# Keys and values of four tiles at once, from thirds of the context on four row groups of the tensor engine

## The chip, the cores and the metric

The kernel runs on one core of one Trainium2 chip. The metric is the device time of one launch in microseconds (us), taken as the median of three runs. TensorE (PE in the profile, with its weight loads as PEld) multiplies, ScalarE (ACT), VectorE (DVE) and GpSimd (POOL) do the rest, and SyncE (SP) issues the DMAs. All data are float32. Each float32 matmul shows as two PE instructions in the trace.

## The reference, cut to what matters

A stack of four layers runs over 128 sequences of 64 tokens with 128 channels. Each layer is a gated cross-attention to a context of 64 tokens with 96 channels, followed by a gated feed-forward part. Layers 0, 1 and 3 have attention of this form:

```python
# heads of 64 channels: 8 in layers 0 and 1, 16 in layer 3
q = norm(x) @ Wq          # 128 -> heads * 64
k = ctx @ Wk              #  96 -> heads * 64
v = ctx @ Wv              #  96 -> heads * 64
a = softmax(q k^T * 64 ** -0.5)      # within one sequence; layer 3 has a null key and value besides
x = x + tanh(gate) * ((a v) @ Wo + bo)
```

Layer 2's attention has 16 heads of 8 channels with biases. Layer 0's feed-forward part mixes 16 experts, layer 2's mixes 32, layer 1's is one 128x128 product in the frequency domain (it is folded into layer 1's attention here), layer 3's is a low-rank MLP.

## The kernel before

The 8192 tokens are 64 tiles of 128. A tile is two sequences. `x` stays in SBUF for the whole kernel; so does the transposed context, `ctxT`, with 96 rows of channels, a row of ones below them, and 8192 columns of tokens.

The stages run one after the other: layer 0's attention (`l0x`), its experts (`l0f`), layer 1's attention with its feed-forward part (`l1x`), layer 2's attention (`l2x`) and experts (`l2f`), layer 3's attention (`l3x`) and MLP (`l3f`). Within a stage the order of every engine is written out by hand: engines are wrapped in `InOrder` (line 158), so each of them executes in the order of the Python calls. DMAs that `load` and `weights` issue on SP are not in that written order. The last steps of a stage call `ahead().step()`, which emits the first steps of the next stage.

`l0x` and `l1x` come from `cross` (line 382). They take the tiles in 32 pairs. Function `periods` (line 354) runs period i, and in it each entry `(lag, f)` of a plan for pair i + lag. In one period of `l0x` the plan gives this order:

- `turn` of pair i-2 (line 284): transposes of the attention weights into two PSUM banks, which ACT copies to `aT`
- `qk` of pair i (line 207): queries (`psq`) and keys (`psk`) by two banks each, copied by ACT with a scale to `qT` and `kT`
- `power` and `divide` of pair i-1 (lines 269 and 273): the exponential on ACT, then on DVE the sums `den` and their reciprocal `rec`, then on POOL the product
- `add` of pair i-3 (line 400): the output projection into a bank `pso`, which DVE takes up in one instruction that adds it to `x`
- `turned` of pair i+1 (line 347): transposes of the normalised tokens (`psx`), copied by ACT
- `values` of pair i (line 219): values into two banks `psv`, copied by ACT
- `scores` and `less` of pair i (lines 231 and 244), then `second` of pair i-2 (line 292): the product of weights and values, which ACT copies to `oT`

`l1x` has besides, between `turned` and `values`, the transposes and the product of the feed-forward part; DVE takes up that product's bank (`ps_l1f`) right after `pso`. `l3x` (line 1146) has the same period for each half (8 heads) of each pair, 64 periods in all; there the projection of the first half is copied by ACT (`y`), that of the second is added by DVE (line 1231), and the null key and value bring two small steps, `null` and `turn_null`.

PSUM has eight banks. `bank` (line 63) hands out single ones from four, and `banks` (line 66) pairs from two pairs; scores and `o` take pairs, and all else takes single ones:

```python
return psum.tile([P, 512], F32, tag="one", name=name, bufs=4)
```

## Time and profile before

| What | us |
|---|---|
| median of three runs | 3196.38 |
| lowest and highest | 3195.07, 3200.67 |
| profiled execution, its own time | 3195.21 |
| span in its profile, first to last instruction | 3193.4 |
| PE busy | 3028.7 |
| DVE busy | 1938.7 |
| ACT busy | 1586.8 |
| POOL busy | 1259.6 |

The profiled execution took 1.8 us more than its span, and 1.2 us less than the median. By the stretches of the trace, `l0x` runs to about 366 us, `l0f` to 930, `l1x` to 1309, `l2x` to 1638, `l2f` to 2401, `l3x` to about 3120 and `l3f` to the end. The PE column of such a table says how long an engine had an instruction under way; it does not say whether the next one could have begun sooner.

### The profile page before, as it was taken

What the parts mean: (1) busy time and instruction counts of PE and PEld (TensorE: products, weight loads), DVE (VectorE), ACT (ScalarE), POOL (GpSimd) and SP (SyncE); (2) the same over time, 40 slices, a digit from 0 to 9 for tenths busy, and PEclk for the clock granted to TensorE, in tenths of its full rate; (3) what the DMA queues carried; (4) which work ended last, traced back from release to release, by engine and by line L of the source; (5) the groups of instructions that cost most, each with busy time, mean ns of one, the idle gap of its engine ahead of it and who ended that gap; (6) DMA issues with size and microseconds to landing.
All of it is one profiled execution on the core that took longest, in us unless ns stands there. A gap on an engine that the chain in (4) does not pass through costs nothing.

```text
span 3193.4 us, 80225 instructions
## 1 busy us (share of the span) xinstructions
PE 3028.7 (95%) x34146; PEld 2023.2 (63%) x34146; DVE 1938.7 (61%) x4589; ACT 1586.8 (50%) x2790; POOL 1259.6 (39%) x1441
## 2 busy tenths in 40 slices
PE   8999999999989999788889999999999999999998
PEld 7887644444448888565654444444447888888883
DVE  5666566666536667699864444444445666666674
ACT  5666432222236666688823233233225666666665
POOL 3434211111014444787624444444442333333343
PEclk9999999999989999999999999999999999999999
DMA  5000455654610000000034534534520000000001
GB/s 150 2 2 2 113 128 116 137 120 112 141 50 2 3 3 2 29 3 2 3 71 90 107 74 87 107 77 84 107 54 13 3 2 2 3 2 2 2 2 54
DMA packets 85672, 165.03 MB, mean 52 GB/s; under 512 B 7393, under 2 KB 16225, under 8 KB 84353
## 3 DMA queue, kind: packets, MB, share of 16 engines
q1 hardware_dynamic: 85314, 159.90, 22.2%
q8 instruction: 268, 4.39, 0.6%
q14 instruction: 90, 0.74, 0.1%
HBM read 154.10 MB, written 5.77 MB: 50 GB/s over the span
## 4 chain that ended last, share of the span: by engine, by line
PE 78%; DVE 12%; ACT 6%; POOL 2%; issue 2%; DMA 0%; SPq 0%; DVEq 0%; ACTq 0%; POOLq 0%
PE psgu_l2f L166 11%; PE psqkv_l0f L166 10%; PE psy_l2f L166 5%; PE pso_l3x L166 4%; PE psq_l3x L166 4%; PE psv_l3x L166 4%; PE psy_l0f L166 4%; PE psk_l3x L166 4%; PE sc_l3x L166 2%; PE psa_l3x L166 2%; PE o_l3x L166 2%; PE psq_l1x L166 2%; PE psv_l1x L166 2%; PE psk_l1x L166 2%; PE psv_l0x L166 2%; PE pso_l1x L166 2%
## 5 line engine op out<-in xcount | busy, mean ns | idle before, releaser
L166 PE MATMUL psgu_l2f<-xT_l2f,w_l2f 128*128 128x512 f32 x1088 | 512.7, 594 | 1.6 <-DVE uw_l2f L166 1.5
L166 POOL TENSOR_TENSOR h_l2f<-uw_l2f,sl_l2f 128x512 f32<-128x512 f32 x256 | 324.9, 1269 | 417.3 <-DVE uw_l2f L166 417.3
L166 ACT ACTIVATE sl_l2f<-psgu_l2f 128x512 f32<-128x512 f32 x272 | 162.4, 597 | 483.8 <-PE psgu_l2f L166 483.6
L166 DVE TENSOR_TENSOR uw_l2f<-psgu_l2f,wb_l2f 128x512 f32<-128x512 f32 x256 | 176.2, 689 | 370.5 <-ACT sl_l2f L166 370.5
L166 PEld LDWEIGHTS psgu_l2f<-xT_l2f,w_l2f 128*128 128x128 f32 x1088 | 202.7, 190 | 239.4 <-issue 225.2
L166 PE MATMUL psqkv_l0f<-xs_l0f,w_l0f 128*128 128x512 f32 (+1 forms) x1024 | 350.2, 599 | 1.8 <-DVE xs_l0f L166 1.7
L166 PE MATMUL psy_l2f<-h_l2f,w_l2f 128*128 128x512 f32 x544 | 277.5, 592 | 0.0
L166 PEld LDWEIGHTS psqkv_l0f<-xs_l0f,w_l0f 128*128 128x128 f32 (+1 forms) x1024 | 124.4, 163 | 187.2 <-issue 177.2
L166 POOL TENSOR_TENSOR at_l3x<-s_l3x,rec_l3x 128x1024 f32<-128x1024 f32 x64 | 121.7, 1902 | 189.4 <-PE psv_l3x L166 96.4
L166 PEld LDWEIGHTS psy_l2f<-h_l2f,w_l2f 128*128 128x128 f32 x544 | 103.3, 190 | 130.2 <-issue 128.2
L166 DVE TENSOR_REDUCE den_l3x<-s_l3x 128x16 f32<-128x1040 f32 x64 | 79.1, 1236 | 155.5 <-ACT s_l3x L166 155.5
L166 POOL TENSOR_SCALAR rs_l0f<-mv_l0f 128x4 f32<-128x4 f32 x16 | 15.2, 950 | 378.4 <-DVE mv_l0f L166 378.4
L166 DVE TENSOR_TENSOR xs_l0f<-wb_l0f,xT_l0f 128x1024 f32<-128x1024 f32 x128 | 151.8, 1215 | 5.1 <-DMA wb_l0f<-wrow_l0f 2.6
L166 POOL TENSOR_TENSOR x<-x,gbias_b 128x256 f32<-128x256 f32 (+1 forms) x80 | 67.9, 849 | 212.9 <-DVE ln_xn_l1x L166 109.3
L166 POOL TENSOR_TENSOR s_l2x<-s_l2x,m_l2x 128x1024 f32<-128x1024 f32 x64 | 120.4, 1903 | 51.8 <-DVE m_l2x L166 29.3
L166 PE MATMUL psq_l3x<-xT_l3x,w_l3x 128*128 128x256 f32 x512 | 136.8, 390 | 2.3
L166 PE MATMUL psk_l3x<-ctxT,w_l3x 96*128 96x256 f32 x512 | 132.8, 381 | 0.0
L166 DVE TENSOR_TENSOR s_l3x<-sc_l3x,maskf_m 128x512 f32<-128x512 f32 x128 | 82.5, 686 | 82.5 <-PE sc_l3x L166 82.5
L166 PE MATMUL pso_l3x<-w_l3x,oT_l3x 128*128 128x128 f32 x1024 | 130.2, 275 | 0.8 <-ACT oT_l3x L166 0.8
L166 PEld LDWEIGHTS pso_l3x<-w_l3x,oT_l3x 128*128 128x128 f32 x1024 | 126.8, 192 | 4.5 <-ACT oT_l3x L166 1.1
L166 PE MATMUL psv_l3x<-w_l3x,ctxT 96*64 96x256 f32 x1024 | 124.6, 385 | 0.0
L166 PE MATMUL psy_l0f<-mix_l0f,w_l0f 128*128 128x512 f32 x256 | 117.1, 611 | 2.0 <-DVE mix_l0f L166 2.0
(564 smaller groups left out, 6789.3 us busy)
## 6 DMA issues: line engine op xcount, KB each, us to landing
wb_l0f<-wrow_l0f SPq DMA_DIRECT2D x256, 256.0 KB, 6.2
wb_l2f<-wrow_l2f SPq DMA_DIRECT2D x128, 512.0 KB, 8.6
out_dram<-x SPq DMA_DIRECT2D x16, 256.0 KB, 2.6
w_l2f<-in_l2f_dram SPq DMA_DIRECT2D x1, 3280.0 KB, 10.3
w_l0f<-in_l0f_dram SPq DMA_DIRECT2D x1, 2120.0 KB, 28.3
w_l3x<-in_l3x_dram SPq DMA_DIRECT2D x1, 2113.0 KB, 8.6
x<-in_x_dram SPq DMA_DIRECT2D x1, 2048.0 KB, 18.7
ctxT<-in_ctxT_dram SPq DMA_DIRECT2D x1, 1536.0 KB, 24.2
```

The costliest lines, as they stand in the source:

```text
L166: got = getattr(self.eng, op)(*args, **kwargs)
```

## The change

Three things change for `l0x`, `l1x` and `l3x`. The context lies in SBUF as `ctx4`: each group of four tiles has its first tile's channels on partitions 0 to 31, the second's on 32 to 63, and so on, and the 96 channels are three thirds of 32, one after another along the free dimension. The weights of keys and values are cut the same way and repeated on the four sets of 32 partitions, so they are three times as wide. The new class `Keys` makes the keys, or the values, of four tiles in one burst: for each third, four matmuls of 32 rows each, one for each tile, on the four row groups, adding up in four PSUM banks. The burst takes all four single banks at once, and then ACT copies the four. Keys are made in odd periods and values in even ones, after `scores` and `less`.

In `l3x` the order of the halves is changed so that two pairs share a burst. Its value and output weights are a new tile `l3v`, loaded at the start of `l2f`. `l2x` needs whole columns of the context, so it loads them again from DRAM in pieces of 512 tokens (`held`), for its mean over the context (now 16 reductions in place of 4) and for its keys and values. The two scales of layer 3's queries and keys are one, on the queries. At the start, the weights of the keys are loaded ahead of those of the queries. The row of ones is not loaded.

```diff
-XA = dict(q=512, k=512, v=512, o=512)
+XA = dict(q=512, k=3 * 512, v=3 * 512, o=512)
...
-    "l3x": Cols(q=1024, k=1024, v=1024, o=1024, gn=1, nv=1, hot=8 * 16),
+    "l3x": Cols(q=1024, k=3 * 1024, gn=1, nv=1, hot=8 * 16),
+    "l3v": Cols(v=3 * 1024, o=1024),
...
-    ctxT = const.tile([DC + 1, NTOK], F32, name="ctxT")
+    ctx4 = const.tile([P, NG, 3, P], F32, name="ctx4")
...
     load(ident, "cst", 0, P)
-    load_w0("q")
     load_row(0, 8 + DM)
     load_ctx(0, 512)
     load_w0("k")
+    load_w0("q")
...
+    class Keys:
...
+        def burst(self, name, pl, bufs, blocks):
+
+            ps = [bank(f"ps{name}_{self.name}_{t}") for t in range(4)]
+            for block in blocks:
+                for c in range(3):
+                    for t in range(4):
+                        for r_out, c_out, lhsT, rhs in block(slice(32 * t, 32 * t + 32), c):
+                            self.pe.matmul(ps[t][r_out, c_out], lhsT=lhsT, rhs=rhs, start=c == 0, stop=c == 2)
+            got = pl.tile([P, 4, 512], F32, tag=f"{name}4", name=f"{name}4_{self.name}", bufs=bufs)
+            for t in range(4):
+                self.act.copy(got[:, t, :], ps[t])
+            return got
+
+        def keys(self):
+
+            def block(j):
+                def parts(rows, c):
+                    c0 = c * self.width + self.off + j * P
+                    return [(slice(0, P), slice(j * P, (j + 1) * P), self.w["k"][rows, c0:c0 + P], ctx4[rows, self.g, c, :])]
+                return parts
+            self.k = self.burst("k", self.wk, 1, [block(j) for j in range(4)]).rearrange("p t (j q) -> p t j q", q=P)
+
+        def values(self):
+
+            def block(b):
+                def parts(rows, c):
+                    c0 = c * self.width + self.off
+                    return [(slice(r * 64, (r + 1) * 64), slice(b * 256, (b + 1) * 256), ctx4[rows, self.g, c, b * SQ:(b + 1) * SQ],
+                             self.w["v"][rows, c0 + r * 256:c0 + (r + 1) * 256]) for r in range(2)]
+                return parts
+            self.v = self.burst("v", self.late, 2, [block(b) for b in range(2)]).rearrange("p t (b k) -> p t b k", b=2)
...
             plan = [
-                (-2, lambda p: H[p].turn()), (1, norm), (0, lambda p: H[p].qk(0, N[p].xT)),
-                (0, lambda p: H[p].qk(1, N[p].xT)), (-1, lambda p: H[p].power()), (2, lambda p: N[p].moments(xp[p])),
-                (-1, lambda p: H[p].divide()), (-3, add), (1, lambda p: N[p].turned()), (0, lambda p: H[p].values()),
-                (0, lambda p: H[p].scores()), (0, lambda p: H[p].less()), (-2, lambda p: H[p].second()),
+                (-2, lambda p: H[p].turn()), (1, norm), (0, lambda p: H[p].queries(N[p].xT)),
+                (-1, lambda p: H[p].power()), (2, lambda p: N[p].moments(xp[p])),
+                (-1, lambda p: H[p].divide()), (-3, add), (1, lambda p: N[p].turned()),
+                (0, lambda p: H[p].scores()), (0, lambda p: H[p].less()), (1, of_two(lambda g: KV[g].keys())),
+                (0, of_two(lambda g: KV[g].values())), (-2, lambda p: H[p].second()),
             ]
...
+            def context(k, g):
+                load(held[k][g % 2][0:DC, :], "ctxT", g * 512, (g + 1) * 512, slice(0, DC))
...
+            for g in range(NG):
+                k = "kv"[g // 2 % 2]
+                dve.tensor_reduce(cm[:, 8 * g:8 * g + 8], held[k][g % 2].rearrange("p (b k) -> p b k", k=SQ), AX.X, ALU.add)
+                if g + 4 < NG:
+                    context(k, g + 4)
...
+            l3v = ctx.enter_context(opened("l3v")).tile([P, LAY["l3v"].n], F32, name="w_l3v")
+            load(l3v, "l3v", 0, LAY["l3v"].n)
...
+        def of(i):
+            return 2 * (i // 4) + i % 2, i // 2 % 2
...
-                (0, lambda i: H[i].qk(0, N[i // 2].xT)), (0, lambda i: H[i].qk(1, N[i // 2].xT)),
+                (0, lambda i: H[i].queries(N[of(i)[0]].xT)),
                 (-1, lambda i: H[i].power()), (2, first(moments)), (4, make), (-1, divide),
-                (-3, project), (1, first(turned)), (0, lambda i: H[i].values()),
-                (0, lambda i: H[i].scores()), (0, lambda i: H[i].less()), (-2, lambda i: H[i].second()),
+                (-3, project), (1, first(turned)), (0, lambda i: H[i].scores()), (0, lambda i: H[i].less()),
+                (1, of_two(lambda n: KV[n].keys())), (0, of_two(lambda n: KV[n].values())), (-2, lambda i: H[i].second()),
```

More of the change, by code (lines that the diff above doesn't have):

```diff
@@ L96, in load_ctx @@
     def load_ctx(lo, hi):
-        load(ctxT[0:DC, lo:hi], "ctxT", lo, hi, slice(0, DC))
+        g0, g1 = lo // 512, hi // 512
+        load(ctx4[:, g0:g1].rearrange("p g c q -> p (g c q)"), "ctx4", g0 * 384, g1 * 384)
     w0 = wpool.tile([P, LAY["l0x"].n], F32, tag="wx", name="w_l0x")
@@ L126, in load_rest @@
             load_ctx(lo, hi)
-        load(ctxT[DC:DC + 1, :], "ctxT", 0, NTOK, slice(DC, DC + 1))
     tg = const.tile([P, 8], F32, name="tg")
@@ L192, in run, with __init__ @@
                 pass
+    class Keys:
+        def __init__(self, engines, wk, late, w, off, width, g, name):
+            self.act, self.pe = engines[1], engines[3]
+            self.wk, self.late, self.w, self.off, self.width, self.g, self.name = wk, late, w, off, width, g, name
+        def burst(self, name, pl, bufs, blocks):
[24 more added lines that the diff above has]
+            self.v = self.burst("v", self.late, 2, [block(b) for b in range(2)]).rearrange("p t (b k) -> p t b k", b=2)
@@ L194, in flamingo_kernel, with __init__ @@
     class Heads:
-        def __init__(self, engines, wk, late, w, off, p, name, qs, ks, mask=None, null=None):
+        def __init__(self, engines, wk, late, w, off, p, name, scale, kv, mask=None, null=None):
             self.dve, self.act, self.pool, self.pe, _ = engines
-            self.home = dict.fromkeys(("aT", "oT", "v", "s"), late)
+            self.home = dict.fromkeys(("aT", "oT", "s"), late)
             self.wk, self.w, self.off, self.p, self.name = wk, w, off, p, name
-            self.scale, self.mask, self.null = dict(q=qs, k=ks), mask, null
+            self.scale, self.kv, self.mask, self.null = scale, kv, mask, null
@@ L204, in new, with queries @@
         def new(self, tag, shape, bufs=1):
             return self.home.get(tag, self.wk).tile(shape, F32, tag=tag, name=f"{tag}_{self.name}", bufs=bufs)
-        def qk(self, half, xT):
-            tok, w, name = self.p * 256, self.w, self.name
-            if half == 0:
-                self.T = {k: self.new(f"{k}T", [P, 4, 256]) for k in "qk"}
-            for k, K, rhs in (("q", P, xT), ("k", DC, ctxT[0:DC, tok:tok + 256])):
-                ps = bank(f"ps{k}_{name}_{half}")
+        def queries(self, xT):
+            self.qT = self.new("qT", [P, 4, 256])
+            for half in range(2):
+                ps = bank(f"psq_{self.name}_{half}")
@@ L213, in qk @@
                 for i in range(2):
                     c0 = self.off + (half * 2 + i) * P
-                    self.pe.matmul(ps[:, i * 256:(i + 1) * 256], lhsT=w[k][0:K, c0:c0 + P], rhs=rhs, start=True, stop=True)
-                self.act.activation(self.T[k][:, 2 * half:2 * half + 2, :].rearrange("p a b -> p (a b)"), ps, AF.Copy,
-                                    scale=self.scale[k])
-        def values(self):
-            self.v = v = self.new("v", [P, 4, 256], bufs=3)
-            for half in range(2):
-                ps = bank(f"psv_{self.name}_{half}")
-                for i in range(2):
-                    b0 = self.p * 256 + (half * 2 + i) * SQ
-                    for r in range(2):
-                        self.pe.matmul(ps[r * 64:(r + 1) * 64, i * 256:(i + 1) * 256], lhsT=ctxT[0:DC, b0:b0 + SQ],
-                                       rhs=self.w["v"][0:DC, self.off + r * 256:self.off + (r + 1) * 256],
-                                       start=True, stop=True)
-                self.act.copy(v[:, 2 * half:2 * half + 2, :].rearrange("p a b -> p (a b)"), ps)
+                    self.pe.matmul(ps[:, i * 256:(i + 1) * 256], lhsT=self.w["q"][:, c0:c0 + P], rhs=xT, start=True, stop=True)
@@ L231, in scores @@
+                self.act.activation(self.qT[:, 2 * half:2 * half + 2, :].rearrange("p a b -> p (a b)"), ps, AF.Copy,
+                                    scale=self.scale)
         def scores(self):
@@ L240, in scores @@
                             self.pe.matmul(sc[b * 64:(b + 1) * 64, r, (t * 4 + j) * 64:(t * 4 + j + 1) * 64],
-                                           lhsT=self.T["q"][rows, j, c0:c0 + SQ], rhs=self.T["k"][rows, j, c0:c0 + SQ],
+                                           lhsT=self.qT[rows, j, c0:c0 + SQ],
+                                           rhs=self.kv.k[rows, 2 * (self.p % 2) + t, j, b * SQ:(b + 1) * SQ],
                                            start=True, stop=True)
@@ L301, in second @@
                                 self.pe.matmul(o[hi * 64:(hi + 1) * 64, r, c0:c0 + 64],
-                                               lhsT=self.v[rows, t * 2 + b, j * 64:(j + 1) * 64],
+                                               lhsT=self.kv.v[rows, 2 * (self.p % 2) + t, b, j * 64:(j + 1) * 64],
                                                rhs=self.aT[rows, t, j, b * 64:(b + 1) * 64], start=True, stop=True)
@@ L345, in scaled, with turned @@
                                        ALU.subtract, ALU.mult)
-        def turned(self, tag="xT", scale=1.0):
+        def turned(self, tag="xT", scale=1.0, bufs=1):
             ps = bank(f"psx_{self.name}")
@@ L350, in turned, with of_two @@
                 self.pe.transpose(ps[:, t * P:(t + 1) * P], self.xn[:, t, :], ident)
-            self.xT = self.new(tag, [P, 256])
+            self.xT = self.new(tag, [P, 256], bufs)
             self.act.activation(self.xT, ps[:, 0:256], AF.Copy, scale=scale)
+    def of_two(f):
+        return lambda i: f(i // 2) if i % 2 == 0 else None
     def periods(n, plan):
@@ L391, in cross @@
             W[nxt] = weights(nxt)
-            H = [Heads(engines, wk, late, w, 0, p, f"{key}_{p}", 0.125, 1.0, mask=mask) for p in range(NP)]
+            KV = [Keys(engines, wk, late, w, 0, 512, g, f"{key}_{g}") for g in range(NG)]
+            H = [Heads(engines, wk, late, w, 0, p, f"{key}_{p}", 0.125, KV[p // 2], mask=mask) for p in range(NP)]
             N = [Norm(engines, wk, f"{key}_{p}") for p in range(NP)]
@@ L451, in mix @@
                     del M[p]
-                plan[9:9] = [(-5, lambda p: M[p].turned("xT2")), (-6, mix)]
-                plan[6:6] = [(-4, begin)]
+                plan[8:8] = [(-5, lambda p: M[p].turned("xT2")), (-6, mix)]
+                plan[5:5] = [(-4, begin)]
                 plan[2:2] = [(-5, lambda p: norm(p, M, "b1f", "ln_xn2"))]
@@ L758, in l2_cross @@
             yield True
-            cm = wk.tile([DC + 1, NB], F32, name="cm", bufs=1)
-            for c in range(4):
-                b0 = slice(c * NB // 4, (c + 1) * NB // 4)
-                dve.tensor_reduce(cm[:, b0], ctxT[:, c * NTOK // 4:(c + 1) * NTOK // 4].rearrange("p (b k) -> p b k", k=SQ),
-                                  AX.X, ALU.add)
-                yield True
+            held = {k: [wk.tile([DC + 1, 512], F32, name=f"ctx_{k}{i}", bufs=1) for i in range(2)] for k in "kv"}
+            for k in "kv":
+                for i in range(2):
+                    gps.memset(held[k][i][DC:DC + 1, :], 1.0)
+            def context(k, g):
+                load(held[k][g % 2][0:DC, :], "ctxT", g * 512, (g + 1) * 512, slice(0, DC))
+            cm = wk.tile([DC + 1, NB], F32, name="cm", bufs=1)
+            for g in range(4):
+                context("kv"[g // 2], g)
+            yield True
+            for g in range(NG):
[3 more added lines that the diff above has]
+                    context(k, g + 4)
+                if g % 4 == 3:
+                    yield True
+            for g in range(2):
+                context("k", g)
+                context("v", g)
             dve.tensor_scalar(cm, cm, 1.0 / SQ, None, ALU.mult)
@@ L810, in qk @@
                 ps = bank(f"psk_l2x_{g}")
-                mat.matmul(ps, lhsT=w["k"][0:DC + 1, :], rhs=ctxT[:, g * 512:(g + 1) * 512], start=True, stop=True)
+                mat.matmul(ps, lhsT=w["k"][0:DC + 1, :], rhs=held["k"][g % 2], start=True, stop=True)
+                if g + 2 < NG:
+                    context("k", g + 2)
                 kT = sg[g]["k"] = wk.tile([P, 512], F32, tag="kT", name=f"kT_l2x_{g}")
@@ L861, in values @@
                 for b in range(4):
-                    b0 = u * 256 + b * SQ
+                    b0 = u % 2 * 256 + b * SQ
                     for r in range(2):
-                        mat.matmul(ps[r * 64:(r + 1) * 64, b * 64:(b + 1) * 64], lhsT=ctxT[:, b0:b0 + SQ],
+                        mat.matmul(ps[r * 64:(r + 1) * 64, b * 64:(b + 1) * 64], lhsT=held["v"][u // 2 % 2][:, b0:b0 + SQ],
                                    rhs=wv[0:DC + 1, r], start=True, stop=True)
                 su[u]["psv"] = ps
+                if u % 2 == 1 and u // 2 + 2 < NG:
+                    context("v", u // 2 + 2)
             def place(u):
@@ L1125, in l2_ffn @@
             yield False
+            l3v = ctx.enter_context(opened("l3v")).tile([P, LAY["l3v"].n], F32, name="w_l3v")
+            load(l3v, "l3v", 0, LAY["l3v"].n)
+            W["l3x"].update(views(l3v, "l3v"))
             with opened("l2f_2", 2) as wk2, opened("l2f_wb", 4, RIGHT) as wbp:
@@ L1179, in l3_cross @@
         H, sn, y, anT = {}, {}, {}, {}
+        def of(i):
+            return 2 * (i // 4) + i % 2, i // 2 % 2
         def of_pair(f):
-            return lambda i: f(i // 2) if i % 2 == 0 else None
+            return lambda i: f(of(i)[0]) if of(i)[1] == 0 else None
         moments = of_pair(lambda p: N[p].moments(xp[p], twice=True))
         scaled = of_pair(lambda p: N[p].scaled(xp[p]))
-        turned = of_pair(lambda p: N[p].turned(scale=w["gn"]))
+        turned = of_pair(lambda p: N[p].turned(scale=w["gn"], bufs=2))
         for f in (moments, scaled, turned):
@@ L1194, in l3_cross @@
             NO = [Norm(engines, wk, f"l3x_{p}o") for p in range(NP)]
+            KV = [Keys(engines, wk, wk, w, 512 * (n % 2), 1024, n // 2, f"l3x_{n}") for n in range(2 * NG)]
             def null(i):
-                p, hf = divmod(i, 2)
+                p, hf = of(i)
                 if hf == 0:
@@ L1203, in null @@
                     actor.copy(sn[p].rearrange("p t h -> p (t h)"), ps[:, 0:32])
-                H[i] = Heads(engines, wk, wk, w, 512 * hf, p, f"l3x_{p}_{hf}", rs, rs, mask=mask, null=sn[p][:, :, 8 * hf:8 * hf + 8])
+                H[i] = Heads(engines, wk, wk, w, 512 * hf, p, f"l3x_{p}_{hf}", rs * rs, KV[i // 2], mask=mask,
+                             null=sn[p][:, :, 8 * hf:8 * hf + 8])
             def divide(i):
-                p, hf = divmod(i, 2)
+                p, hf = of(i)
                 H[i].divide(ans[p % 2][:, :, 8 * hf:8 * hf + 8])
             def turn_null(i):
-                p, hf = divmod(i, 2)
+                p, hf = of(i)
                 if hf == 1:
@@ L1220, in project @@
             def project(i):
-                p, hf = divmod(i, 2)
+                p, hf = of(i)
                 more = [(anT[p][:, t * P:(t + 1) * P], nvo) for t in range(2)] if hf == 1 else (None, None)
@@ L1235, in out_ @@
             def out_(i):
-                p, hf = divmod(i, 2)
+                p, hf = of(i)
                 if hf == 1:
@@ L1411, in _o_rows, with _thirds @@
     return m.reshape(2, 2, 2, 64, P).transpose(0, 3, 2, 1, 4).reshape(P, 512)
+def _thirds(m):
+    return np.tile(m.reshape(3, 32, -1).transpose(1, 0, 2).reshape(32, -1), (4, 1))
 def _layout(i):
@@ L1416, in _layout @@
     f["x"] = i["x"].reshape(NT, P, DM).transpose(1, 0, 2).reshape(P, NT * DM)
-    f["ctxT"] = np.concatenate([i["ctx_768"].reshape(NTOK, DC).T, np.ones((1, NTOK), np.float32)])
+    f["ctxT"] = i["ctx_768"].reshape(NTOK, DC).T
+    f["ctx4"] = i["ctx_768"].reshape(NG, 4, P, 3, 32).transpose(1, 4, 0, 3, 2).reshape(P, NG * 3 * P)
     for name, key in (("m0", "mask_BxS2_bk0"), ("m1", "mask_BxS2_bf1")):
         f[name] = i[key].reshape(NT, 2, SQ).transpose(1, 0, 2).reshape(2, NT * SQ)
-    f["l0x"] = _pack("l0x", q=i["L0_xattn_W_q"], k=i["L0_xattn_W_k"], v=_v_cols(i["L0_xattn_W_v"]),
+    f["l0x"] = _pack("l0x", q=i["L0_xattn_W_q"], k=_thirds(i["L0_xattn_W_k"]), v=_thirds(_v_cols(i["L0_xattn_W_v"])),
                      o=_o_rows(i["L0_xattn_W_o"]))
-    f["l1x"] = _pack("l1x", q=i["L1_xattn_Wq"], k=i["L1_xattn_Wk"], v=_v_cols(i["L1_xattn_Wv"]),
+    f["l1x"] = _pack("l1x", q=i["L1_xattn_Wq"], k=_thirds(i["L1_xattn_Wk"]), v=_thirds(_v_cols(i["L1_xattn_Wv"])),
                      o=_o_rows(i["L1_xattn_Wo"]))
@@ L1458, in _layout @@
     nk, nv = i["L3_xattn_null_kv"]
-    f["l3x"] = _pack("l3x", q=i["L3_xattn_Wq"], k=wkv[:, :1024],
-                     v=np.concatenate([_v_cols(wkv[:, c:c + 512]) for c in (1024, 1536)], axis=1),
-                     o=np.concatenate([_o_rows(wo[c:c + 512]) for c in (0, 512)], axis=1),
+    f["l3v"] = _pack("l3v", v=_thirds(np.concatenate([_v_cols(wkv[:, c:c + 512]) for c in (1024, 1536)], axis=1)),
+                     o=np.concatenate([_o_rows(wo[c:c + 512]) for c in (0, 512)], axis=1))
+    f["l3x"] = _pack("l3x", q=i["L3_xattn_Wq"], k=_thirds(wkv[:, :1024]),
                      gn=i["L3_xattn_g_norm"][:, None], nv=np.concatenate([nv, nv])[:, None], hot=hot.reshape(P, -1))
```

## The prediction, made before the changed kernel was run

> **What bounds the kernel now.** I read the page first, then the stages, then one period of `l0x` in order of time.

> ```profile
> PE 3028.7 (95%) x34146; PEld 2023.2 (63%) x34146; DVE 1938.7 (61%) x4589; ACT 1586.8 (50%) x2790; POOL 1259.6 (39%) x1441
> ```

> By stretches of the span (length, then busy time of PE, PEld, DVE, ACT, POOL with instructions, PE clock, DMA share, GB/s), and by groups of PE instructions:

> ```profile
> 40.00:335.00 295.00, 288.58 (x5062) 246.62 (x5062) 185.95 (x397) 190.33 (x311) 120.62 (x150) 0.99 0.02 6
> ```

> ```profile
> L166 PE MATMUL psv_l0x<-w_l0x,ctxT 96*64 96x256 f32 x512 | 62.3, 385 | 0.0
> ```

> PE is under way in 288.6 of 295 us of `l0x`, and the values found PE idle for 0.0 us. No transfer matters there (DMA share 0.02). So the stage is a row of matmuls. The period says how long each takes, and where the other engines stand (start, duration, engine):

> ```profile
> 202.15 1.01 ACT L166 COPY oT_l0x<-o_l0x 128x1024 f32<-128x1024 f32 x1 [1.51 <-PE o_l0x L166]
> ...
> 203.05 1.08 ACT L166 COPY aT_l0x<-psa_l0x 128x512 f32<-128x512 f32 x2
> ...
> 203.75 1.03 PE L166 MATMUL psk_l0x<-ctxT,w_l0x 96*128 96x256 f32 x4
> ...
> 204.01 0.63 ACT L166 ACTIVATE qT_l0x<-psq_l0x 128x512 f32<-128x512 f32 x1
> ...
> 204.61 1.03 PE L166 MATMUL psq_l0x<-xT_l0x,w_l0x 128*128 128x256 f32 x4
> ...
> 206.34 1.95 PE L166 MATMUL pso_l0x<-w_l0x,oT_l0x 128*128 128x128 f32 x16
> 206.54 0.60 ACT L166 ACTIVATE kT_l0x<-psk_l0x 128x512 f32<-128x512 f32 x1 [0.27 <-PE psk_l0x L166]
> ...
> 207.04 1.05 ACT L166 ACTIVATE s_l0x<-s_l0x 128x1024 f32<-128x1024 f32 x1
> ...
> 208.12 1.22 DVE L166 TENSOR_REDUCE den_l0x<-s_l0x 128x16 f32<-128x1024 f32 x1 [1.96 <-ACT s_l0x L166]
> 208.13 0.38 PE L166 MATMUL psx_l0x<-cst_t,ln_xn_l0x 128*128 128x128 f32 x2
> ...
> 208.44 1.95 PE L166 MATMUL psv_l0x<-w_l0x,ctxT 96*64 96x256 f32 x16
> ...
> 209.61 0.39 DVE L166 SCALAR_TENSOR_TENSOR x<-pso_l0x,tg,x 128x256 f32<-128x256 f32 x1
> ...
> 210.32 1.16 PE L166 MATMUL sc_l0x<-kT_l0x,qT_l0x 64*64 64x64 f32 x64
> ```

> Four PE instructions of 256 columns take 203.75 to 204.61, so 0.216 each; sixteen of 128 columns take 206.34 to 208.13, 0.112 each. Keys are 8 x 0.216 = 1.73 us of a period, values 208.44 to 210.32 = 1.88. The start of `sc` recurs every 10.39 us here; read the same way, every 11.06 in `l1x`, and by turns 10.39 and 11.54 (mean 10.97) in `l3x`. The second thing to see: DVE frees the bank of `pso` only at 210.00, 1.5 us after PE has gone on to the values. Today nobody waits for it, since other single banks are free.

> **The change part by part: PE.** A burst of keys is 4 blocks x 3 thirds x 4 tiles = 48 matmuls, 96 instructions of 128 columns; of values, 2 x 3 x 4 x 2 = 48, so 96 of 256 columns. What they cost hangs on overlap. The trace has row groups of 32 at work:

> ```profile
> 3120.20 1.14 PE L166 MATMUL psh_l3f<-pT_l3f,w_l3f 32*128 32x512 f32 x8
> ...
> 1340.74 1.12 PE L166 MATMUL sc_l2x<-kb_l2x,qT_l2x 32*64 32x256 f32 x32
> ...
> 3185.47 1.72 PE L166 MATMUL psy_l3f<-w_l3f,qT_l3f 32*128 32x128 f32 x32 [0.69 <-ACT qT_l3f L166]
> ```

> Eight of `psh` end in 1.14 us, where a pair of the same length takes 1.02 (`psy_l2f`): four run at once. The 32 of `sc_l2x`, with two column groups besides, end in 1.12 = 4 waves of 0.216 and a tail: eight at once. So keys are 24 waves x 0.112 = 2.69, values 12 x 0.216 = 2.59, and 0.2 us for filling and changing over: about 2.83 for either. [...] With the rows, PE alone has 2 x (1.73 + 1.88) = 7.22 us per two periods before and 2.69 + 2.59 + 0.4 = 5.68 after: -1.54 x 64 = -99 us. No more is in it: 96 rows in four row groups of 32 are three quarters of the passes.

> **ACT and PSUM.** The copies are as many and as large as before, and two scales on ACT become plain copies: nothing. [...] A burst needs all four single banks within its first four matmuls, so each earlier user must have been taken up, `pso` among them; and its four copies all begin after its end. Behind them on ACT, in written order, stand `oT`, two of `aT`, two of `qT`, then the exponential; behind that on DVE `den`, `rec` and the taking up of `pso`; and then the next burst. Laid out from the end of a burst in `l0x`, by the starts above: 0.25 to the first copy; four copies 4 x 0.48 = 1.92; `oT` 0.90; `aT` 0.96; `qT` 2 x 0.50; the exponential 1.08 until `den`; `den` to the end of the adding 1.88; 0.1 to PE. That is 8.1 us. PE meanwhile has 10.39 - 1.73 - 1.88 = 6.8 us of work, so it stands for 1.3 us in each period. Loop: 8.1 + 2.83 = 10.92 against 10.39, +0.53 x 32 = +17 us. In `l1x`, `ps_l1f` is taken up 0.39 us after `pso`: 8.5 + 2.83 = 11.31 against 11.06, +8 us. In `l3x` only two periods of four have the adding on DVE (den to its end 2.07, and `anT` and `sn` on ACT 0.4 to 0.6): 11.7 and 11.5; in the other two PE has 9.9 and about 10.3, as the queries wait for banks that `aT` frees late (3.6 us after the burst, where PE comes at 2.5 to 3.4). The mean, 10.9, is that of before less 0.1; waits that this leaves out could add 0.3. I take 0, between -7 and +13 us. While PE waits for the banks, `second` and the transposes behind it wait too, and so ACT's `oT`, which is in the loop already.

> **Weights and context.** The rows for transfers, SP's issues in order of time and then size and time to landing:

> ```profile
> 348.77 3.96 SPq L166 DMA_DIRECT2D wb_l0f<-wrow_l0f  x6
> 366.28 0.35 SPq L76 DMA_DIRECT2D w_l1x<-in_l1x_dram  x1
> 366.68 7.64 SPq L166 DMA_DIRECT2D wb_l0f<-wrow_l0f  x10
> ```

> ```profile
> w_l3x<-in_l3x_dram SPq DMA_DIRECT2D x1, 2113.0 KB, 8.6
> ...
> w_l1x<-in_l1x_dram SPq DMA_DIRECT2D x1, 1024.0 KB, 5.2
> ```

> At the start 1 MB more is needed before the first values: at the 271 GB/s of the first 40 us 3.9 us, of which the idle 10 us of PE there hide some: +3 (0 to 5). `w_l1x` doubles and stands ahead of ten fetches of `wb_l0f`, for which DVE waits at the start of `l0f` already: +3 (0 to 5). `l3v`, 2 MB, can land only where `oT_all` lay, after its last product near 1638, just when `l2f` waits for its first `wb_l2f`. If SP takes it first, that is 8 us (the row of `w_l3x`); but the rows above show SP issuing six fetches ahead of a load that stands earlier in the program and was not ready. I take +2 (0 to 8). In `l2x` 48 loads of 192 KB land in 3.8 us by the row of `ctxT`; each is issued two groups, some 15 us, ahead, on a queue with nothing urgent behind it while the load waits for its tile, so 0 (if each of 32 were bare, 120 us). The 16 reductions add about 1 us on DVE in the tail of `l1x`, beside PE work. Four memsets on POOL: 0. Sum: +8.

> **Sum.** 17 + 8 + 0 + 8 = +33 us on the profiled execution's 3195.2, so 3228; the median stands 1.2 above: 3229, said as 3230. 0.2% (6.4 us) is about what a measurement of this kernel can tell from no change.

> **The rivals.** *PE stays the bound.* If the banks are free when PE gets there, -99 + 8 gives 3195 - 91 = 3104, or 3105 as a median. It is decided by the loop's 8.1 us: below 7.56 in `l0x` the period is shorter than before, at 6.8 the wait is gone; in `l1x` the margin is 0.25, and in `l3x` there is none, so it comes first there. For it: copies in the trace follow each other at 0.46 to 0.50, the exponential could start sooner where PE is early. Against it: the loop is made of ACT and DVE work in a written order, and a faster PE shortens none of it. Half of it, a loop 0.5 us shorter everywhere, gives 3230 - 64 = 3166. Chance of the end below 3190: 0.14.

> *The waves do not overlap as `sc_l2x` does.* [...] If only two row groups ran at once, both bursts would take 5.4 us and each of the 128 periods 2.6 more: 3230 + 333 = 3563. `psy_l3f`, which steps through pairs of row groups, takes 1.72 for 32, against 3.6 for one group at a time. Chance 0.14, nearly all of it the mild form.

> *The change comes out even*, the loop giving back just what PE saves: within 3190 to 3203, 0.08.

> The forecast, with 0.64, has its own range: a loop of 7.9 to 8.4 us, `l3x` from -7 to +13, transfers from 0 to 16: 3204 to 3268. The range is 3188 to 3290: below it 0.12, above it about 0.07. Faster by more than 0.2% 0.14, within 0.2% 0.08, slower 0.78.

> **What would show it.** Right: in `l0x` PE idle before the first matmul of nearly every burst, some 1.3 us, released by DVE's adding of `pso`; `sc` recurring at about 10.9 in `l0x` and 11.3 in `l1x`; ACT's four copies back to back after a burst; PE busy time falling by tens of us while the span grows. Wrong: no idle before bursts and `sc` at 9.6 in `l0x` (rival one); bursts well over 3 us from first to last matmul (rival two); a gap of 8 us at the start of `l2f` (`l3v` first in the queue); PE waiting for `held` in `l2x`.

## The result and the profile after

The changed kernel takes 3211.73 us (median of 8 runs, 3207.06 to 3215.5) against 3196.68 of the kernel before beside it: ratio 1.0044, 95% interval 1.0032 to 1.0056, so 15 us slower. The profiled execution took 3213.53 us, its span is 3211.8 (before: 3195.21 and 3193.4). The forecast was slower, at 3230, that is +33 us: the sign came out, the size is less than half. It put the three loops 33 us too long and the stretches between them 19 us too short, which the total alone hides.

The page's line of busy time of the kernel after, and then its stretch of `l0x` by windows (length, busy time of PE, PEld, DVE, ACT, POOL, PE clock, DMA share, GB/s):

```profile
PE 3012.8 (94%) x43362; PEld 2046.0 (64%) x43362; DVE 1923.7 (60%) x4601; ACT 1526.0 (48%) x2790; POOL 1263.4 (39%) x1445
```

```profile
40.00:335.00 295.00, 285.19 (x6931) 250.53 (x6930) 180.80 (x389) 174.13 (x306) 118.53 (x144) 0.98 0.01 3
```

PE's busy time fell by only 16 us, although by the prediction's estimate the bursts hold 99 us less of passes. An instruction that waits inside a burst counts as under way (the burst below is under way for 3.62 us, one without a wait in experiment 1 for 2.85), so "94% busy" says even less here than before; one has to look at the period. The timeline of `l0x`, in the kernel after, shows a period with a burst of values and the next burst, of keys:

```profile
203.61 1.16 PE L168 MATMUL sc_l0x<-k_l0x,qT_l0x 64*64 64x64 f32 x64
...
204.70 0.22 PEld L168 LDWEIGHTS psv_l0x<-w_l0x,ctx 32*64 32x64 f32 x12
204.70 3.62 PE L168 MATMUL psv_l0x<-w_l0x,ctx 32*64 32x256 f32 x96
...
205.06 0.39 DVE L168 SCALAR_TENSOR_TENSOR x<-pso_l0x,tg,x 128x256 f32<-128x256 f32 x1
...
205.50 2.35 PEld L168 LDWEIGHTS psv_l0x<-w_l0x,ctx 32*64 32x64 f32 x84 [0.59 <-DVE x L168]
...
207.96 2.05 ACT L168 COPY v_l0x<-psv_l0x 128x512 f32<-128x512 f32 x4 [3.81 <-PE psv_l0x L168]
...
208.24 1.16 PE L168 MATMUL o_l0x<-aT_l0x,v_l0x 64*64 64x64 f32 x64
...
209.87 1.06 ACT L168 COPY oT_l0x<-o_l0x 128x1024 f32<-128x1024 f32 x1
...
210.78 1.14 ACT L168 COPY aT_l0x<-psa_l0x 128x512 f32<-128x512 f32 x2
211.73 1.17 ACT L168 ACTIVATE qT_l0x<-psq_l0x 128x512 f32<-128x512 f32 x2
...
212.69 1.14 ACT L168 ACTIVATE s_l0x<-s_l0x 128x1024 f32<-128x1024 f32 x1
...
213.87 1.22 DVE L168 TENSOR_REDUCE den_l0x<-s_l0x 128x16 f32<-128x1024 f32 x1 [3.59 <-ACT s_l0x L168]
...
215.36 0.39 DVE L168 SCALAR_TENSOR_TENSOR x<-pso_l0x,tg,x 128x256 f32<-128x256 f32 x1
...
215.81 2.75 PEld L168 LDWEIGHTS psk_l0x<-ctx,w_l0x 32*128 32x128 f32 x90 [0.32 <-DVE x L168]
...
218.58 2.05 ACT L168 COPY k_l0x<-psk_l0x 128x512 f32<-128x512 f32 x4 [3.94 <-PE psk_l0x L168]
218.68 1.49 PE L168 MATMUL o_l0x<-aT_l0x,v_l0x 64*64 64x64 f32 x64
```

This is the predicted loop, link by link: burst, four copies, `oT`, `aT`, `qT`, exponential, `den`, taking up of `pso`, next burst. But the burst is in two parts. Twelve weight loads run at 204.70; the other 84 come only at 205.50, released by DVE's `x`. And ACT's copies begin at 207.96, before PE has gone on from the burst to `o` at 208.24; after the burst of keys, at 218.58 for 218.68.

Stages and seams, from the start of the first or last named matmul in the two profiled executions (differences of the time of the stretch, us). One execution is a thin base for the small ones: `l0x` has the same code in the changed kernel, experiments 4 and 5 and the first two kernels of 6, and there it takes 335.6 to 338.2 us.

| stretch | before | after | difference | forecast |
|---|---|---|---|---|
| start to first `sc_l0x` | 14.0 | 15.6 | +1.6 | +3 |
| `l0x`, first to last `sc` (period 10.39, then 10.46) | 333.5 | 338.2 | +4.7 | +17 |
| last `sc_l0x` to first `psqkv_l0f` | 20.5 | 30.6 | +10.1 | +3 |
| `l0f`, to first `sc_l1x` | 574.3 | 575.9 | +1.6 | 0 |
| `l1x`, first to last `sc` (11.06, then 10.86) | 337.4 | 330.6 | -6.8 | +8 |
| last `sc_l1x` to first `sc_l2x` | 29.5 | 36.6 | +7.1 | 0 |
| `l2x` and `l2f`, to first `sc_l3x` | 1098.3 | 1100.3 | +2.0 | +2 |
| `l3x`, first to last `sc` (mean 10.97, then 10.93) | 692.5 | 686.3 | -6.2 | 0 |
| last `sc_l3x` to first `psy_l3f` | 41.2 | 45.4 | +4.2 | 0 |

The three loops together are 8 us shorter, where +25 was forecast; the stretches between them are 27 us longer, where +8 was. So the sign was luck in part: the loops, which were to make the kernel slower, made it quicker, and the seams, hardly reckoned with, made it slower.

### The profile page after: what moved, and what is told of

The parts are those of the page before. It is cut to its first block, busy times and chain, and to the rows that moved or that the text cites. A ratio compares the mean times of both kernels' runs of the same rounds, so it can differ in the third digit from the quotient of the medians.

```text
span 3211.8 us, 98752 instructions
## 1 busy us (share of the span) xinstructions
PE 3012.8 (94%) x43362; PEld 2046.0 (64%) x43362; DVE 1923.7 (60%) x4601; ACT 1526.0 (48%) x2790; POOL 1263.4 (39%) x1445
## 4 chain that ended last, share of the span: by engine, by line
PE 65%; DVE 14%; ACT 14%; issue 4%; POOL 2%; DMA 1%; SPq 0%; DVEq 0%; ACTq 0%; POOLq 0%
PE psgu_l2f L168 11%; PE psqkv_l0f L168 11%; PE psy_l2f L168 5%; PE psy_l0f L168 4%; PE psq_l3x L168 3%; PE psv_l3x L168 3%; PE pso_l3x L168 3%; PE psk_l3x L168 3%; PE psk_l1x L168 2%; PE psq_l1x L168 2%; PE psk_l0x L168 2%; PE pso_l1x L168 2%; PE sc_l3x L168 2%; PE psv_l1x L168 2%; ACT k_l3x L168 1%
## 5 line engine op out<-in xcount | busy, mean ns | idle before, releaser
L168 PE MATMUL psqkv_l0f<-xs_l0f,w_l0f 128*128 128x512 f32 (+1 forms) x1024 | 353.1, 602 | 12.6 <-DVE xs_l0f L168 12.5
L168 DVE TENSOR_TENSOR xs_l0f<-wb_l0f,xT_l0f 128x1024 f32<-128x1024 f32 x128 | 151.6, 1215 | 14.2 <-DMA wb_l0f<-wrow_l0f 11.7
L168 PE MATMUL psq_l3x<-xT_l3x,w_l3x 128*128 128x256 f32 x512 | 132.8, 394 | 14.8 <-ACT aT_l3x L168 10.8
L168 PE MATMUL pso_l3x<-w_l3v,oT_l3x 128*128 128x128 f32 x1024 | 131.2, 277 | 0.8 <-ACT oT_l3x L168 0.8
L168 PEld LDWEIGHTS pso_l3x<-w_l3v,oT_l3x 128*128 128x128 f32 x1024 | 128.1, 194 | 4.2 <-ACT oT_l3x L168 1.1
L168 ACT COPY k_l3x<-psk_l3x 128x512 f32<-128x512 f32 x128 | 65.8, 601 | 132.2 <-PE psk_l3x L168 132.2
L168 ACT COPY v_l3x<-psv_l3x 128x512 f32<-128x512 f32 x128 | 65.8, 601 | 126.0 <-PE psv_l3x L168 126.0
L168 PEld LDWEIGHTS psq_l3x<-xT_l3x,w_l3x 128*128 128x128 f32 x512 | 90.6, 192 | 36.6 <-ACT aT_l3x L168 27.2
## 6 DMA issues: line engine op xcount, KB each, us to landing
w_l2f<-in_l2f_dram SPq DMA_DIRECT2D x1, 3280.0 KB, 11.1
w_l3x<-in_l3x_dram SPq DMA_DIRECT2D x1, 2113.0 KB, 7.8
```

The costliest lines, as they stand in the source:

```text
L168: got = getattr(self.eng, op)(*args, **kwargs)
```

## Experiments

Ratios are to the kernel before on the same chip, whose median was 3200.76 us beside experiments 1 and 5, the first attempt of 3 and the first kernel of 6; 3200.5 beside experiment 4, the second attempt of 3 and the other two kernels of 6; and 3198.24 beside experiments 2 and 7.

**1. Is it the order on DVE that holds the bursts?** In `l0x` and `l1x` the taking up of `pso`, and of `ps_l1f`, is issued ahead of `den`:

```
-  (-1, lambda p: H[p].divide()), (-3, add), (1, lambda p: N[p].turned()),
+  (-3, add), (1, lambda p: N[p].turned()), (-1, lambda p: H[p].divide()),
-  plan[8:8] = [(-5, lambda p: M[p].turned("xT2")), (-6, mix)]
+  plan[7:7] = [(-5, lambda p: M[p].turned("xT2")), (-6, mix)]
```

> In the two stages made by cross, DVE takes up pso (and ps_l1f) before it sums den; nothing else is changed. If the loop burst, four copies, oT, aT, qT, exponential, den, pso taken up, next burst sets the period, den and the exponential drop out of it and PE becomes the bound: sc recurs at 9.6 to 9.7 us in l0x (10.46 in the changed kernel) and at 10.2 to 10.4 in l1x (10.86); -25 and -16 us, so about 3170. Rival, PE itself sets the period since the bursts do not overlap as far as the rows of before showed: both periods stay within 0.1 and the time stays at 3212.

3182.68 us, ratio 0.994 (0.9917 to 0.9964). The periods fall to 9.77 in `l0x` and 10.44 in `l1x`; `l3x`, which has its own plan, keeps its own. That is somewhat less than expected (9.6 to 9.7, 10.2 to 10.4, about 3170). Its timeline in `l0x`:

```profile
209.85 0.48 DVE L168 SCALAR_TENSOR_TENSOR x<-pso_l0x,tg,x 128x256 f32<-128x256 f32 x1 [3.01 <-PE pso_l0x L168]
...
209.97 1.16 PE L168 MATMUL sc_l0x<-k_l0x,qT_l0x 64*64 64x64 f32 x64
...
210.25 1.21 DVE L168 TENSOR_REDUCE den_l0x<-s_l0x 128x16 f32<-128x1024 f32 x1
...
211.06 2.39 PEld L168 LDWEIGHTS psv_l0x<-w_l0x,ctx 32*64 32x64 f32 x96
211.06 2.85 PE L168 MATMUL psv_l0x<-w_l0x,ctx 32*64 32x256 f32 x96
```

`x` is done while PE is still at the scores, and the burst goes through in one piece (x96, no wait, 2.85 us). So the bound of the changed loops in `l0x` and `l1x` was the order of three instructions on DVE, not PE's work.

**2. Does the same edit help without bursts?** The edit alone, in the kernel before.

> The kernel before, with the one edit of e1_take_up_first alone: the take-up of the projection ahead of the softmax's sum on DVE in l0x and l1x. Theory (before the change PE is the bound of these loops and no burst waits for the take-up's bank, so the order on DVE costs nothing there): periods of 10.39 and 11.06 us unchanged within 0.1, total within 6 us of the kernel before. Rival (the order costs the kernel before as much as the changed one, and e1_take_up_first's gain has nothing to do with the change): periods shorter by 0.4 to 0.7 us, total lower by 20 to 40 us.

3211.89 us, ratio 1.0039 (1.0026 to 1.0052): slower. The rival falls; the theory's "unchanged" missed too, since the period grew from 10.39 to 10.47 in `l0x` and from 11.06 to 11.35 in `l1x`. Its timeline in `l1x`, and then the same transposes in the kernel before, which wait for nothing:

```profile
1149.95 0.48 DVE L166 SCALAR_TENSOR_TENSOR x<-ps_l1f,tg,x 128x256 f32<-128x256 f32 x1 [0.40 <-PE ps_l1f L166]
...
1150.35 1.21 DVE L166 TENSOR_REDUCE den_l1x<-s_l1x 128x16 f32<-128x1024 f32 x1
...
1154.04 1.09 PE L166 MATMUL psa_l1x<-cst_t,s_l1x 128*128 128x128 f32 x8 [0.23 <-POOL s_l1x L166]
```

```profile
1149.30 1.09 PE L166 MATMUL psa_l1x<-cst_t,s_l1x 128*128 128x128 f32 x8
```

Here `den` stands behind two additions that wait for PE and begins 2.58 us after the start of the exponential, where it was 1.08; the division on POOL comes later, and the transposes wait for it. In these loops the order that suits the kernel before is the opposite of the one that suits bursts over four banks.

**3. Why is the loop shorter than forecast?** Reading: tiles 0 to 2 have their banks early and run two waves ahead, while tile 3 waits for the bank of `pso`; they finish two waves (2 x 0.216 us) early, and their copies need not wait for the burst's end. A first attempt put tile 3 first in both loops of `burst`:

```
-  for t in range(4):      (matmuls, and copies)
+  for t in (3, 0, 1, 2):
```

> Each burst begins with tile 3, whose bank (that of pso in l0x) is free last, and ACT copies tile 3 first; nothing else is changed. In the changed kernel tiles 0 to 2 run two waves ahead while tile 3 waits, so that ACT's first copy starts before the burst has ended. If this head start is what the prediction left out, it is gone here: all four tiles end together, the first copy starts 0.2 to 0.3 us after the burst, and the period of l0x goes from 10.46 to about 10.9, the 10.92 of the prediction; about +14 us in l0x, up to +10 in each of l1x and l3x, 3225 to 3245. Rival, another term of the loop was mis-sized (copies or oT shorter than taken): the period stays within 0.1 of 10.46.

3211.38 us, ratio 1.0038 (1.0026 to 1.0049), period 10.46 as before. This did not take the head start away (copies at 206.07, `o` at 206.36), so it tells nothing of the reading. It looks as if the bank that comes free late goes to whichever tile is used last, not to a tile number; this is not shown. The second attempt left the matmuls alone and gave only the copies that order, so that ACT's first copy needs the late tile:

> The bursts' four copies on ACT start with tile 3, the bank that comes free last, then 0, 1, 2; the matmuls keep their order, and nothing is left out. Theory (the copies begin before the burst's end because tiles 0 to 2 run two waves ahead of tile 3, so the copies cost about 0.5 us less than the prediction charged): the first copy now waits for tile 3's end, the l0x period goes from 10.46 to between 10.8 and 11.0, the l1x period from 10.86 to between 11.1 and 11.3, and the total grows by 15 to 35 us over the changed kernel, that is to 3227 to 3247 us. Rival (PE's own work or the end of the whole burst sets the period, the copies' start does not): periods unchanged within 0.05 us and the total at 3212 us.

3237.91 us, ratio 1.0112 (1.0093 to 1.0131), some 22 us over the changed kernel by the ratios. The periods are 10.76 in `l0x` (10.70 and 10.83 by turns; forecast of the prediction 10.92) and 11.16 in `l1x` (11.31). Its timeline:

```profile
208.51 0.39 DVE L168 SCALAR_TENSOR_TENSOR x<-pso_l0x,tg,x 128x256 f32<-128x256 f32 x1
...
208.95 2.35 PEld L168 LDWEIGHTS psv_l0x<-w_l0x,ctx 32*64 32x64 f32 x84 [0.80 <-DVE x L168]
...
211.69 1.16 PE L168 MATMUL o_l0x<-aT_l0x,v_l0x 64*64 64x64 f32 x64
...
211.80 2.05 ACT L168 COPY v_l0x<-psv_l0x 128x512 f32<-128x512 f32 x4 [4.41 <-PE psv_l0x L168]
```

The copies now begin 0.11 us after the start of `o`, not 0.28 before it: 0.39 us later, where two waves of values are 0.43. After a burst of keys they begin 0.11 after it as well, not 0.10 before: 0.21 later, where two waves of keys are 2 x 0.112 = 0.22. The other links of the loop keep their lengths. A change of a few tenths of a microsecond on ACT moved the whole loop: the head start is what the prediction missed. And even without it the first copy comes sooner than the 0.25 us that the prediction took. In the kernel before, the second copy of values had shown that, 0.12 us after the start of the scores at 210.32:

```profile
210.44 0.59 ACT L166 COPY v_l0x<-psv_l0x 128x512 f32<-128x512 f32 x1 [0.28 <-PE psv_l0x L166]
```

**4. Is `l3x` held in the same way?** The same order there:

```
-  (4, make), (-1, divide), (-3, project), (1, first(turned)), (0, lambda i: H[i].scores()),
+  (4, make), (-3, project), (1, first(turned)), (-1, divide), (0, lambda i: H[i].scores()),
```

> In l3x alone, the softmax's sum and division of the half before are issued behind the projection and the turned input, not ahead of them. Nothing is left out. Theory (in l3x, as in l0x, the in-order queue of DVE holds the take-up of the projection behind the sum, and with it the bank that the next burst's last tile needs): the periods with a burst behind them, 11.61 and 11.23 us, fall by 0.3 to 0.8 us each, the mean from 10.93 to 10.5, the total by 10 to 30 us to 3182 to 3202 us. Rival (l3x is bound by the chain of softmax and weights through DVE and POOL, so a later sum only makes the division and the transposes late): the mean rises to 11.0 to 11.6 and the total to 3214 to 3255 us.

3200.96 us, ratio 1.0 (0.9987 to 1.0013), some 14 us below the changed kernel by the ratios. The four periods went from 11.61, 11.23, 10.24, 10.64 to 11.61, 10.87, 9.71, 10.64, mean 10.71: the direction and the sum were expected, the place only in part. 11.61 did not move and 10.24 did, so what sets the longest period of `l3x` is not this order. What it is was not tried.

**5. The start of `l0f`.** In the kernel after, SP's issues and who waits for them:

```profile
371.88 0.34 SPq L77 DMA_DIRECT2D w_l1x<-in_l1x_dram  x1
...
372.41 13.42 SPq L168 DMA_DIRECT2D wb_l0f<-wrow_l0f  x12
...
383.11 1.23 DVE L168 TENSOR_TENSOR xs_l0f<-wb_l0f,xT_l0f 128x1024 f32<-128x1024 f32 x1 [10.73 <-DMA wb_l0f<-wrow_l0f]
...
384.38 2.08 PE L168 MATMUL psqkv_l0f<-xs_l0f,w_l0f 128*128 128x512 f32 x2 [12.54 <-DVE xs_l0f L168]
```

Before, six fetches had been issued at 348.77 and only ten stood behind `w_l1x`; now all stand behind it, and it is twice as large (2048 KB for 1024). PE waits 12.54 us. The experiment moves `W["l1x"] = weights("l1x")` behind `fetch(1)`:

> The load of layer 1's attention weights (2 MB) is issued after the first two fetches of l0f, instead of ahead of them. PE idles 12.5 us there in the changed kernel, until the first wb_l0f lands. If the 2 MB ahead in the queue are the cause, the idle time falls to 2 to 6 us and the time by 7 to 10 us. If the place of wb_l0f in SBUF, which is free late, is the cause, the fetches are issued at the same moment and only some 4 us are won.

3212.27 us (one run). Its timeline at the same place:

```profile
370.69 12.45 SPq L168 DMA_DIRECT2D wb_l0f<-wrow_l0f  x16
...
375.70 1.23 DVE L168 TENSOR_TENSOR xs_l0f<-wb_l0f,xT_l0f 128x1024 f32<-128x1024 f32 x1 [4.62 <-DMA wb_l0f<-wrow_l0f]
```

PE's wait falls from 12.54 to 6.43 us, and the seam from 30.6 to 24.5 (24.9 with the same edit in experiment 7; before: 20.5). So 6 of the 10 us are the 2 MB ahead of the fetches. The other 4 remain with fetches issued at 370.69 instead of 348.77; in the kernel after SP waits 42.6 us there, at the load of `w_l1x`, for the last `pso_l0x` on PE, where in the kernel before its first fetch waited 29.2 us for scores (`sc_l0x`). That this is because the place in memory that the fetches land in is free later is argued. The total did not follow: the last scores of `l3x` came 6 us earlier, but `l3f` took 48.1 us instead of 44.2. Experiment 6 shows how that can happen.

**6. The seams to `l2x` and to `l3f`.** First the written order: `l2x`'s front two periods of `l1x` earlier (start `NP - 8` for `NP - 6`).

> The first steps of l2x begin two periods of l1x earlier. From the last sc of l1x to the first of l2x the changed kernel takes 36.6 us where before took 29.5. If that is the one step more that the context loads add to the front of l2x, it falls to 27 to 31 and the time by 5 to 9 us. If it is the loads or the 16 reductions themselves that hold up DVE, the stretch gets shorter by less than 2 us, or l1x gets longer by as much.

3211.89 us (one run), and the gap is 36.3 us: a miss. It tells something else: the 16 reductions over the context are done by 1274 there, before the last scores at 1289, while in the changed kernel four of them come after the last scores, and the gap is nearly the same. So their place alone does not explain it. What the profile does show at both seams is PE's clock. PE in the kernel after, at the start of `l2x` and in the tail of `l3x`:

```profile
1312.86 0.60 PE L168 MATMUL psx_l2x<-cst_t,xn_l2x 128*128 128x128 f32 x4
1316.51 0.66 PE L168 MATMUL psx_l1f<-cst_t,ln_xn_l1f 128*128 128x128 f32 x2 [3.06 <-DVE ln_xn_l1f L168]
...
1317.82 1.92 PE L168 MATMUL psq_l2x<-xT_l2x,w_l2x 128*128 128x512 f32 x2
```

```profile
3126.12 1.97 PE L168 MATMUL psa_l3x<-cst_t,at_l3x 128*128 128x128 f32 x8 [4.29 <-POOL at_l3x L168]
```

In the kernel before, the same queries of `l2x`:

```profile
1302.12 1.02 PE L166 MATMUL psq_l2x<-xT_l2x,w_l2x 128*128 128x512 f32 x2
```

The granted clock by windows in the kernel after (the number ahead of the last two):

```profile
1316.00:1318.00 2.00, 1.49 (x7) 1.51 (x8) 0.60 (x2) 0.00 (x0) 1.75 (x5) 0.50 0.43 178
1318.00:1320.00 2.00, 2.00 (x4) 0.83 (x3) 0.48 (x1) 0.61 (x2) 0.62 (x1) 0.50 0.00 0
...
3124.00:3128.00 4.00, 1.88 (x9) 1.88 (x10) 0.18 (x1) 0.58 (x1) 2.06 (x2) 0.54 0.01 2
```

Two matmuls of 512 columns take 1.92 us, where the kernel before has 1.02, with its clock at 1.00; eight transposes take 1.97, elsewhere 1.04 to 1.09. The next kernel fills the two waits with repeats that write the same values again:

```
-  for t in range(4):                                   (transposes of l2x)
+  for t in list(range(4)) * (6 if g == 0 else 1):
-  for t in range(2):                                   (second)
+  for t in list(range(2)) * (3 if self.name == "l3x_30_1" else 1):
```

> Repeats that write the same values again: the four transposes of the first l2x group run six times, and the weighted values of one late l3x half three times, so that PE is busy in the waits of 3.05 and 4.29 us after which the granted clock stood at 0.50. Theory (the longer transitions l1x to l2x and l3x to l3f, 36.6 against 29.5 us and 45.4 against 41.2 us, come from PE's clock, halved after an idle stretch that the kernel before didn't have): the clock stays near 1.00 there, the matmuls of queries and keys at l2x's start take 1.02 us for two instead of 1.92, and the two gaps fall to 31 to 33 and 42 to 43.5 us, the total by 5 to 8 us to about 3205 us. Rival (the gaps come from the chain of DVE and POOL at the seam, and the clock only accompanies it): both gaps unchanged or longer by up to 2 us each, total 3212 to 3216 us.

3209.94 us, ratio 1.0022 (1.0014 to 1.0029). Its windows:

```profile
1316.00:1320.00 4.00, 3.11 (x16) 1.89 (x15) 1.08 (x3) 1.78 (x4) 3.04 (x6) 1.00 0.42 171
...
3124.00:3128.00 4.00, 2.45 (x20) 2.31 (x21) 0.00 (x0) 1.60 (x4) 1.50 (x1) 1.00 0.01 2
```

The clock stays at 1.00 in both places, and more work makes the kernel quicker. The gaps fall from 36.6 to 34.9 and from 45.4 to 43.3. So the clock accounts for half of what the second seam lost (2.1 of 4.2), but for less than expected of the first (1.7 of 7.1): there the clock fell at another place instead, 0.70 from 1302 to 1306, in this execution. The rest of that gap stays open. These shares are rough: in the nine traces with bursts and no repeats the first gap runs from 36.3 to 39.3 and the second from 44.7 to 46.0, so the repeats may be worth 1.4 to 4.4 us at the first and 1.4 to 2.7 at the second. The same repeats on top of the first experiment:

> The take-up of the projection ahead of the sum in l0x and l1x (as in e1_take_up_first) together with the repeats of e7_pe_kept_busy. Theory of the clock: the gap from the last scores of l1x to the first of l2x, 39.3 us in e1_take_up_first, falls by 3 to 7 us and the total from 3182.7 to about 3177 us. If the gap there comes from the chain of DVE and POOL: 3182 to 3186 us.

3178.64 us, ratio 0.9926 (0.9911 to 0.994): the first gap fell from 39.3 to 35.4 as expected and the median by 4 us, but the intervals of the two kernels overlap, and `l3f` took 46.8 us instead of 44.2, with the clock at 0.63 to 0.81 in three of its stretches. At the second seam the repeats did not hold the clock this time. First the kernel with the repeats alone, then this one:

```profile
3125.55 1.09 PE L168 MATMUL psa_l3x<-cst_t,at_l3x 128*128 128x128 f32 x8 [2.44 <-POOL at_l3x L168]
```

```profile
3089.05 1.97 PE L168 MATMUL psa_l3x<-cst_t,at_l3x 128*128 128x128 f32 x8 [2.44 <-POOL at_l3x L168]
```

The wait is the same, the speed behind it is not, and the gap is 44.7 us instead of 43.3. So the gap follows the clock there, and the length of the wait alone does not decide.

**7. The best version.** Both orders together, and then with `l1x`'s weights later as well:

> The take-up ahead of the sum in all three stages: e1_take_up_first and e5_l3x_divide_later in one kernel. If the two gains add, which they do where each stage is bound by its own loop: a ratio of about 0.990 to the kernel before, some 3168 us against 3200. If what one gains is given back at the seams: 0.993 to 0.995.

3171.01 us, ratio 0.9913 (0.9899 to 0.9928): 0.0131 below the changed kernel, most of the sum of the two gains, 0.0148.

> e10_both_orders with l1x's weights fetched behind l0f's first two gathers, as in e3_l1x_weights_later. l0f's start comes 5 to 6 us earlier, as there. If that stays: a ratio of 0.988 to 0.989. If the clock's halvings at other seams take it back, as in e3_l1x_weights_later: no difference from e10_both_orders within 0.1%.

3164.98 us, ratio 0.9891 (0.9874 to 0.9908): 1.1% quicker than the kernel before. The last edit is worth 6 us by the medians, as expected, though the intervals of the two overlap a little. So the kernel with bursts is the quicker one, once the queues are written for them. How much of the 1.1% the bursts alone bring is not separated: the order of experiment 1 was tried in the kernel before and hurt it, that of experiment 4 and the later weights were not.

## Why the prediction was right and wrong, point by point

- **The waves.** Right. From the release by `x` to `o` a burst takes 2.74 us (values) or 2.87 (keys), and 2.85 in one piece (values, experiment 1); 2.83 was forecast. The rows of the kernel before decided rightly, and the rival of waves that overlap less is out: no run shows its mild form, to which nearly all of its chance of 0.14 went; keys at 2.87 us are their 24 waves of 0.112, 2.69, and 0.18 more.
- **PSUM by order.** Right: the wait before a burst is released by DVE's `x` (0.59 and 0.32 us on PEld), and taking its cause away gains 33 us by the ratios. It was announced as 1.3 us on PE; the profile shows less, because the loop is half a microsecond shorter than forecast and because part of the wait lies inside a burst.
- **The loop of 8.1 us in `l0x`.** The failed step is its first term, "0.25 to the first copy", with the sentence that a burst's "four copies all begin after its end". Measured from the start of `o`, which follows the burst, in the rows above: -0.28 to the first copy, then 1.91, 0.91, 0.95, 0.96, 1.18 to `den`, 1.88 to the end of `x`, 0.06: 7.57 us after a burst of values. After a burst of keys the first copy stands at -0.10 and the loop is 7.75. With the bursts' 2.74 and 2.87 us this gives 10.46 in the mean, the period measured. All other terms hold within 0.1. The prediction wrote that a burst needs all four banks "within its first four matmuls", and did not ask what the three tiles that have theirs do meanwhile: they go ahead. With the head start taken away the term is +0.11, the loop 7.96, and the periods are 10.70 and 10.83 by turns, forecast 10.92. So the term was off by 0.44 us in the mean. The head start is 0.30 of it; the other 0.14 was to be read in the kernel before, whose copy began 0.12 us after the next matmuls (last row of experiment 3). The periods came out 0.46 us below the forecast in `l0x` and 0.45 in `l1x` (10.86 for 11.31): times 32 each, 29 us (27 by the table).
- **`l3x`.** Right as a mean, 10.93 for "that of before less 0.1", but in part by luck. The two periods with the adding on DVE are 11.61 and 11.23 for 11.7 and 11.5, the other two 10.24 and 10.64 for 9.9 and 10.3: errors that cancel. And the reason given for the longest, the adding on DVE behind `den`, does not hold: experiment 4 took it away, and 11.61 stayed.
- **Transfers.** The start (+1.6 for +3), `l2f` (SP did issue two fetches ahead of `l3v`, then the other six) and the loads of `l2x` are right. Wrong is `w_l1x` ahead of the fetches, +3: the seam is 10 longer, since the prediction kept the six early fetches of the kernel before, and they came late as well.
- **Seams.** The 7 us between `l1x` and `l2x` and the 4 between `l3x` and `l3f` were not in the sum. It had no line for what happens when PE idles longer at a seam; the clock is part of it, shown above, and the rest of the first seam is open.
- **The rivals.** "PE stays the bound", at 3104 and in its half form at 3166, is out for this kernel; that the kernel with both orders and the later weights comes to 3165 is not the half form come true, as its edits differ. The decisive length, 7.56 us, was named well: the loop came out at 7.57 and 7.75 by turns, and the period of `l0x` is 0.07 us longer than before.

The sum by the table: 33 - 27 (`l0x` and `l1x`) - 6 (`l3x`) + 19 (the seams) = +19, where the spans differ by 18.4 and the medians by 15. The two errors met: more than half of what the wrong term took off was put back by the seams, of which `l0f`'s had a term that was too small and two had none.

## What to carry to other kernels

When work is packed into bursts over several PSUM banks, look up for every bank who empties it, and move that instruction ahead of any longer one on its queue: here that is worth 33 us by the ratios, twice the 14 that the bursts cost, and in this kernel without bursts the same move hurts (ratio 1.0039). Where a burst waits for one bank, ask what the others do meanwhile, since the consumers of the early ones may start before the burst ends (here ACT's first copy stood 0.28 us before `o` after a burst of values). And give every seam between stages a line of its own in the sum: transfers that lose their place in the queue, and idle stretches of PE: with two of them, of 3.06 and 4.29 us, the clock stood at 0.50 here.
